# Another order of the first loads and of the first value portions in a two-layer decoder

## The chip, the core and the metric

The kernel runs on one core of a Trainium2 chip. A core has four engines that compute, each with its own list of instructions that it works off in order: TensorE (PE, matrix products), VectorE (DVE), ScalarE (ACT) and GpSimd (POOL). They wait for one another through semaphores. A fifth, SyncE (SP), does nothing here but ask for transfers between the chip's memory and the on-chip memory; ACT asks for some as well. Both share 16 DMA engines. The results of matmuls land in a small accumulation memory (PSUM) of eight banks, and have to be read out by ACT or DVE before a bank can be used again.

The metric is the time of one execution on the device, in microseconds (us); lower is better. Several executions of the kernel are timed, and one more is recorded by the profiler.

## The reference

The reference is a decoder of two layers over four batches of 256 tokens with 256 features, and a context of 1601 vectors of 256 features per batch. Cut to what matters here:

```python
x = x + L0_attn(layernorm(x))             # causal self-attention, 16 heads of 16
x = x + L0_xattn(layernorm(x), ctx, mask) # attention over the 1601 context vectors
x = x + L0_ffn(layernorm(x))              # ternary weights, 256 -> 1024 -> 256
x = x + L1_attn(layernorm(x))             # gated recurrence in chunks of 32
x = x + L1_xattn(layernorm(x), ctx)       # 16 heads of 128, 4 groups of keys and values
x = x + L1_ffn(layernorm(x))              # 8 experts, 2 per token
```

Inside `L1_xattn` the keys and values come from the context and the tokens together:

```python
kv_in = concatenate([context_hidden, draft_hidden], axis=1)   # 1601 + 256 rows
k = (kv_in @ Wk.T).reshape(b, total_len, KVH, HD)
v = (kv_in @ Wv.T).reshape(b, total_len, KVH, HD)
```

The values of the context rows depend on nothing but inputs. So they can be computed at any time before the second layer's attention over the context.

## The kernel before

**Two parts.** In the first part (to about 500 us) the four batches pass through the first layer and the recurrence. In the second part the 32 pairs of heads of the second layer's attention over the context follow one another, with the experts worked in between.

**An order written by hand, and a scheduler.** Each stage of a batch is a Python generator that emits a few instructions and yields. The loop at the end of the kernel counts ticks: in each tick every batch that has begun (`START`: batch 0 at tick 0, then at ticks 3, 8 and 13) takes one step, and then the fillers take theirs. A scheduler in the build then sets the order of each engine's instructions out of what was emitted. `behind(gen)` takes one step of a generator, and holds each compute instruction of this step behind the last one emitted before it on the same engine (`keep_behind`). This fixes an order alone and adds no wait.

**Value portions.** The filler that the change touches is `values_ahead(False)` (`ahead`, lines 323 to 349). It first asks for the value weights `wv` (two transfers of 256 KB, in runs of 512 bytes). Then for each context chunk of three batches (four chunks a batch: three of 512 rows and a last one of 65) it asks for the transposed chunk `vcT` (512 KB, into one of three buffers), and works through its portions of 128 rows. A portion is the product `vah` = chunk times `wv` on PE (L344, written as two products, which the profile shows as four matmuls of 512 columns), the copy `vst` out of PSUM by ACT (L347), and a store `v` to memory asked for by SP (L348). There are 13 portions per batch, 39 in all. `FILL` (line 42) tells how many the loop draws in a tick: two in each of the ticks 1 to 13, then one in each, up to tick 33. The first draw also issues the requests for `wv` and the first chunk.

**The start of a batch.** `self_attention(b)`: tick 0 takes the mean and variance of the tokens `x` (L244, L245), and a power on POOL (L268). Tick 1 makes the normed tokens `xh` on ACT (L296). Tick 2 transposes them on PE (`tp_sa`, L304), and DVE and ACT scale the result into `xqkv` (L431, L433). Ticks 3 and 4 make queries and keys (`pq` on PE, L441), which DVE adds to a bias (`qk`, L445). Then values (`pv`, L451; `values`, L456), and, mostly on DVE, the rotation and norm of queries and keys (L469 to L493). Then two transposes (`tp_q`, `tp_k`), a small product for the mask (`xpm`, L620, which needs `mf`, L615), and, for four quarters of the heads in turn, scores (`sc`, L525 and L531), maxima (`mx`, L535), exponentials (`sm`, L543), transposes (`tpp`, `tpq`; copied by ACT into `pT`, L552), the product with the values (`po`) and a last transpose (`tb`, L577).

**First requests.** Before the loop, SP is asked for the tokens of batch 0 (`x`, 256 KB), the weights `wqkv` (768 KB), the tokens of batches 1 to 3 (256 KB each) and `wo0` (256 KB); ACT is asked for the constants `cst` in two pieces (193 and 388 KB), `cols` (11 KB), the broadcast `rows` in two pieces (384 and 256 KB) and two rows of norm weights (`qnw` and `knw`, 64 KB each). The requests of both engines go round over eight completion semaphores, so that each waits until the request eight places before it has landed.

**PSUM.** Portions, transposes and small products draw their banks from one ring of four (`p1`); a bank comes free when the fourth one before has been read out. The scores of a quarter take two double banks (`p2`).

Of the kernel before, what the change touches and what calls it, by code (L numbers as in the profile page):

```python
# [10 lines left out]
F32 = mybir.dt.float32  # L11
# [9 lines left out]
P = 128  # L21
# [8 lines left out]
NKV, REP, HD1 = 4, 4, 128  # L30
# [8 lines left out]
LATE = tuple((3, i) for i in range(4))  # L39
LTICK = 80  # L40
WTICK = 34
FILL = {t: 2 if t < 14 else 1 for t in range(1, 34)}
SIDEN = 2
RATE = 1
START = (0, 3, 8, 13)
# [70 lines left out]
def decoder_kernel(ctx: ExitStack, tc: tile.TileContext, at, t, out):  # L116
# [3 lines left out]
    const = ctx.enter_context(tc.tile_pool(name="const", bufs=1))  # L120
# [16 lines left out]
    def p1(name):  # L137

        ring[0] += 1
        if psb and ring[0] % 3 == 0:  # L140
            return psb[0].tile([P, 512], F32, tag="one", name=name, bufs=2)
        return psa.tile([P, 512], F32, tag="one", name=name, bufs=4)
# [25 lines left out]
    def db(name):  # L168

        return wk.tile([P, 1024], F32, tag="db", name=name, bufs=NDB)  # L170
# [20 lines left out]
    def load_x(b):  # L191
        nc.sync.dma_start(out=xs[b], in_=t["x"][b].rearrange("(j p) d -> p j d", p=P))

    n_const = t["consts"].shape[1]
    cst = const.tile([P, n_const], F32, tag="cst", name="cst")
    soon = at["ones"][0]

    def load_consts(lo, hi):
        nc.scalar.dma_start(out=cst[:, lo:hi], in_=t["consts"][:, lo:hi])
# [25 lines left out]
    def row(r, name):  # L225
        o, n = _ROWS[name]
        nc.scalar.dma_start(out=r[:, 0:n], in_=t["rows"][:, o : o + n].to_broadcast([P, n]))
        return r[:, 0:n]
# [78 lines left out]
    def w512(tag, name):  # L307
        return fr.tile([P, 512], F32, tag=tag, name=name, bufs=2 if tag == "ropu" else NROPE)

    def odd(tag, name):  # L310
        return fr.tile([P, 2 * FF], F32, tag=tag, name=name)
# [7 lines left out]
    def units(i):  # L319

        return (4, 512) if i < 3 else (1, S2 - 12 * P)

    def values_ahead(late):

        if late:
            wv = [fr.tile([P, 512], F32, tag="sum", name=f"wvl{c}", bufs=2) for c in range(2)]
        else:
            w = odd("w3", "wv")
            wv = [w[:, 512 * c : 512 * (c + 1)] for c in range(2)]
        for c in range(2):  # L330
            nc.sync.dma_start(
                out=wv[c].rearrange("p (g n) -> p g n", g=NKV),
                in_=t["wkv1"][c * P : (c + 1) * P].rearrange("p (g two n) -> p g two n", g=NKV, two=2)[:, :, 1, :],
            )
        for b, i in (LATE if late else EARLY):
            n, w = units(i)
            cT = db(f"vcT{b}{i}")[:, 0 : 2 * w].rearrange("p (c n) -> p c n", c=2)
            nc.sync.dma_start(out=cT, in_=t["ctxT"][b][:, i * 512 : i * 512 + w].rearrange("(c p) n -> p c n", p=P))
            kept_values[b, i] = dram.tile([n, P, 512], F32, tag=f"v{b}{i}", name=f"v{b}{i}")
            for k in range(n):  # L340
                r = min(P, w - k * P)
                pv = p1(f"vah{b}{i}{k}")
                for c in range(2):
                    T.matmul(pv[0:r, :], lhsT=cT[:, c, k * P : k * P + r], rhs=wv[c], start=c == 0, stop=c == 1)  # L344
                nm = f"vst{b}{i}{k}"
                st = w512("rope", nm)
                A.copy(st[0:r, :], pv[0:r, :])  # L347
                nc.sync.dma_start(out=kept_values[b, i][k, 0:r, :], in_=st[0:r, :])  # L348
                yield


    def fw(name, k, n, eng, tag):
        n0 = (k // P) * n
        w = w512(tag, name) if n0 == 512 else fr.tile([P, n0], F32, tag=tag, name=name)
        return weight(w, name, 0, k, 0, n, eng)
# [3 lines left out]
    for lo, hi in ((0, 768), (768, 1280)):  # L359
        nc.scalar.dma_start(out=rows[:, lo:hi], in_=t["rows"][:, lo:hi].to_broadcast([P, hi - lo]))  # L360
    bqkv, bo, dtb = rows[:, 0:768], rows[:, 768:1024], rows[:, 1024:1280]
    for b in range(1, B):
        load_x(b)
    load_consts(soon, n_const)
    wo0 = fw("wo0", D, D, nc.sync, "rope")
    qnw, knw = (row(const.tile([P, HD1], F32, tag=n, name=n), n) for n in ("qnw", "knw"))
    identb = fr.tile([P, P], BF16, tag="identb", name="identb")
    G.tensor_copy(identb, ident)

# [7 lines left out]
    def shared_weights():  # L377

        for w in (first_weights["wfc"], first_weights["wpj"]):
            nm = f"g{len(gam)}"  # L380
            w2 = w.rearrange("p c n -> p (c n)")
            part = sm([P, 1], "gpart", f"part{nm}")
            V.tensor_reduce(part, w2, AX.X, ALU.add, apply_absolute_value=True)
            pg = p1(f"pg{nm}")
            T.matmul(pg[:, 0:1], lhsT=cc("ones"), rhs=part, start=True, stop=True)
            gw = fr.tile([P, 1], F32, tag=nm, name=nm)
            V.tensor_scalar(gw, pg[:, 0:1], 1.0 / (FF * D), None, ALU.mult)
            hi = sm([P, 1], "ghi", f"hi{nm}")
            V.tensor_scalar(hi, gw, 1e-6, 0.5, ALU.add, ALU.mult)
            lo = sm([P, 1], "glo", f"lo{nm}")  # L390
            V.tensor_scalar(lo, hi, -1.0, None, ALU.mult)
            gam.append(gw)
            yield
            for i in range(2):
                wi = w2[:, i * 1024 : (i + 1) * 1024]
                neg = db(f"neg{nm}{i}")
                V.tensor_scalar(neg, wi, lo, None, ALU.is_lt)
                V.scalar_tensor_tensor(wi, wi, hi, neg, ALU.is_gt, ALU.subtract)
                yield
        hmr = fr.tile([P, 2, 16], F32, tag="hmr", name="hmr")  # L400
        nc.scalar.dma_start(out=hmr, in_=t["hmrep"])
        for c in range(2):
            V.tensor_mul(
                kron[:, c, :].rearrange("p (m d) -> p m d", d=16), hmr[:, c, :, None].to_broadcast([P, 16, 16]),
                cc("dmask")[:, None, :].to_broadcast([P, 16, 16]),
            )
        yield
# [653 lines left out]
    def run(gen):  # L1061
        for _ in gen:
            pass
# [184 lines left out]
    def before_head(b, g):  # L1248

        if g == 0:  # L1250
            if b == 0:
                yield from angles(b)
            yield from tables(b)
        late = None
        for i in (1, 2, 3):
            gen = prep_kv(b, g, i)
            next(gen)
            yield
            if late:
                run(late)  # L1260
                yield
            late = gen
        run(late)
        yield "context"
        late = None
        if g == 0:
            normed_tokens(b)
            bt[b]["xh"] = bt[b]["centred"]()
            yield
            token_features(b)  # L1270
        for gen in (prep_q(b, g, 0), prep_q(b, g, 1), prep_kv(b, g, 0)):
            next(gen)
            yield
            if late:
                run(late)
                yield
            late = gen
        run(late)
# [215 lines left out]
    first = before_head(0, 0)  # L1494
    first_weights = {}
    tern = shared_weights()
    ahead, late = values_ahead(False), values_ahead(True)
    gens = [before(b) for b in range(B)]
    work = steps()
    through, tick, step, said = [False] * B, 0, 0, None  # L1500
    while not all(through):
        for b, gen in enumerate(gens):
            if tick >= START[b] and not through[b]:

                stage = (behind if b and tick < START[b] + 2 else next)(gen, "through")
                through[b] = stage == "through"
                if stage == "attended" and b == B - 1:

                    win = fw("win", D, 768, nc.sync, "w1")
                    wout = fw("wout", D, D, nc.sync, "rope")  # L1510
                    second_part()
        for _ in range(FILL.get(tick, 0)):
            next(ahead, None)
        if tick >= LTICK:
            next(late, None)
        if tick == WTICK:
            run(ahead)
            first_weights["wfc"] = fw("wfc", D, FF, nc.sync, "w3")
            first_weights["wpj"] = fw("wpj", FF, D, nc.sync, "w4")
        if tick >= TERN:  # L1520
            behind(tern)
        if through[0] and psb:
            if said != "first":
                said = next(first, "first")
            else:
                for _ in range(RATE):
                    if step < 8 and through[1 + step // 4]:
                        step = next(work) + 1
        elif tick >= SIDE and tick % SIDEN == 0 and said != "context":
            said = behind(first)  # L1530
        tick += 1
# [76 lines left out]
```

## Time and profile before

| what | us |
|---|---|
| median of three timed executions | 1777.13 (1775.59 to 1780.58) |
| the profiled execution's own time | 1775.81 |
| its span, first to last instruction | 1774.0 |
| busy: PE | 1708.0 (96%) |
| busy: DVE | 1300.2 (73%) |
| busy: ACT | 994.4 (56%) |
| busy: POOL | 867.2 (49%) |

The page divides the span into 40 equal slices of 44 us; each digit is the busy share of an engine in tenths. The first six slices of PE and of the DMA engines:

| slice | 1 | 2 | 3 | 4 | 5 | 6 |
|---|---|---|---|---|---|---|
| PE, tenths | 6 | 9 | 8 | 9 | 9 | 8 |
| DMA share, tenths | 6 | 3 | 2 | 1 | 2 | 3 |
| GB/s moved | 229 | 118 | 82 | 60 | 78 | 97 |

PE is the busiest engine in the sum, and almost without a gap in the second part. A share over the whole span says nothing of a single stage, though: whether a change in the first part counts is read from the waits of that part, and from what PE does at the times named. Times in the views run from the first instruction of the execution. "Idle before" is the time in which an engine had nothing to do ahead of an instruction, with what ended it; "issue" there means that the profile shows no wait that explains it. The clock column is the share of PE's full clock that was granted.

### The profile page before, as it was taken

To read this page: it belongs to the slowest core of one execution; us is meant where nothing else is said; L and a number is where in the kernel's file an instruction comes from. 1 tells how busy PE (TensorE), PEld (TensorE's weight loads), DVE (VectorE), ACT (ScalarE), POOL (GpSimd) and SP (SyncE) were. 2 spreads that over 40 slices of the span, in tenths; PEclk is the share of its full clock that TensorE was granted. 3 is DMA by queue.
4 is the path that set the end of the run, shared out by engine and by line. 5 is a ranking of instruction groups with operands and counts; after the bars stand their busy time and mean duration, and the time that the engine had idled before them with its cause. 6 is when DMAs were issued, how large, how long until landed. Compare 5 with 4: busy or idle time off the path is not lost.

```text
span 1774.0 us, 20918 instructions
## 1 busy us (share of the span) xinstructions
PE 1708.0 (96%) x6792; PEld 1014.8 (57%) x6792; DVE 1300.2 (73%) x2420; ACT 994.4 (56%) x1741; POOL 867.2 (49%) x719
## 2 busy tenths in 40 slices
PE   6989989988999999999999999999999999999998
PEld 3545668755555555555555656555555555555557
DVE  3663475789658778787787788787778778777675
ACT  2457653555556756567565556656555556655551
POOL 1210023311116677666776565676665656667460
PEclk9999999999999999999999999999999999999999
DMA  6321234201141111121211212131212213111102
GB/s 229 118 82 60 78 97 129 75 6 46 63 134 47 45 60 35 53 59 52 64 40 60 69 42 75 39 102 32 68 46 65 70 35 110 31 51 46 54 1 66
DMA packets 106565, 116.91 MB, mean 66 GB/s; under 512 B 9664, under 2 KB 80468, under 8 KB 106456
## 3 DMA queue, kind: packets, MB, share of 16 engines
q1 hardware_dynamic: 105160, 114.02, 21.0%
q10 hardware_dynamic: 1296, 1.54, 0.3%
q8 instruction: 55, 0.90, 0.2%
q14 instruction: 54, 0.44, 0.1%
HBM read 101.38 MB, written 14.16 MB: 65 GB/s over the span
## 4 chain that ended last, share of the span: by engine, by line
PE 74%; DVE 8%; ACT 7%; POOL 6%; issue 3%; DMA 1%; ACTq 0%; POOLq 0%; SPq 0%; DVEq 0%
PE bpo L1350 19%; PE bsc L1304 19%; PE pk L1233 7%; PE vah L344 4%; POOL sum L1341 3%; PE bpw L1376 3%; PE mph L1008 3%; ACT s L1329 2%; PE pq L1194 2%; ACT s L1305 2%; PE xpo L695 1%; PE mpe L1021 1%; PE xsc L650 1%; PE sc L531 1%; PE tpk L1244 1%
## 5 line engine op out<-in xcount | busy, mean ns | idle before, releaser
L1341 POOL TENSOR_TENSOR sum<-sum,s 128x512 f32<-128x512 f32 (+1 forms) x411 | 533.5, 1298 | 84.8 <-ACT s L1329 59.0
L1304 PE MATMUL bsc<-qTb,kTb 128*128 128x512 f32 (+1 forms) x960 | 457.5, 597 | 2.3 <-ACT kTb L1246 2.3
L1350 PE MATMUL bpo<-s,vb 128*128 128x512 f32 (+1 forms) x960 | 458.8, 596 | 0.0
L1305 ACT ACTIVATE s<-bsc,kn 128x512 f32<-128x512 f32 (+1 forms) x480 | 317.4, 684 | 232.3 <-PE bsc L1304 217.4
L1309 DVE SCALAR_TENSOR_TENSOR acc<-bsc,kn,acc 128x512 f32<-128x512 f32 x448 | 334.3, 746 | 103.3 <-ACT s L1305 88.5
L1326 DVE TENSOR_TENSOR s<-s,bc 128x1024 f32<-128x1024 f32 (+1 forms) x256 | 289.8, 1145 | 14.5 <-PE bc L1322 14.4
L1329 ACT ACTIVATE s<-s 128x1024 f32<-128x1024 f32 (+1 forms) x256 | 256.4, 1006 | 51.7 <-DVE s L1326 50.0
L1304 PEld LDWEIGHTS bsc<-qTb,kTb 128*128 128x128 f32 (+1 forms) x960 | 174.3, 187 | 186.1 <-issue 134.6
L1350 PEld LDWEIGHTS bpo<-s,vb 128*128 128x128 f32 (+1 forms) x960 | 169.1, 191 | 131.8 <-issue 129.5
L1151 POOL TENSOR_TENSOR ropek<-ropek,ropuk 128x512 f32<-128x512 f32 (+1 forms) x64 | 77.0, 1203 | 182.4 <-DVE ropuk L1146 181.3
L1332 POOL TENSOR_TENSOR sum<-s 128x512 f32<-128x512 f32 x32 | 40.9, 1277 | 186.4 <-ACT s L1329 186.4
L1233 PEld LDWEIGHTS pk<-wkv,cTk 128*128 128x128 f32 x832 | 101.6, 192 | 9.2 <-issue 4.5
L1158 ACT ACTIVATE ropeq<-ropeq,rnq 128x128 f32<-128x128 f32 x128 | 41.2, 390 | 113.3 <-POOL rnq L1154 109.7
L1233 PE MATMUL pk<-wkv,cTk 128*128 128x128 f32 x832 | 103.3, 275 | 0.0
L344 PE MATMUL vah<-wv,vcT 128*128 128x512 f32 (+1 forms) x156 | 79.4, 646 | 13.8 <-DMA vcT<-in_ctxT 10.1
L1307 DVE TENSOR_SCALAR acc<-bsc,kn 128x512 f32<-128x512 f32 x32 | 24.0, 750 | 64.8 <-ACT s L1305 64.8
L1376 PEld LDWEIGHTS bpw<-wo,aT 128*128 128x128 f32 x256 | 49.6, 194 | 34.5 <-issue 23.5
L1154 POOL TENSOR_TENSOR kn<-ssk,nhalf 128x4 f32<-128x4 f32 (+1 forms) x64 | 64.9, 1014 | 8.9 <-DVE ssk L1153 8.9
L347 ACT COPY vst<-vah 128x512 f32<-128x512 f32 (+1 forms) x52 | 30.3, 588 | 69.0 <-PE vah L344 50.9
L1376 PE MATMUL bpw<-wo,aT 128*128 128x256 f32 x256 | 67.3, 387 | 0.0
L1151 POOL TENSOR_TENSOR ropeq<-ropeq,ropuq 128x512 f32<-128x512 f32 x32 | 43.8, 1368 | 47.5 <-ACT s L1305 35.5
L1144 ACT ACTIVATE squares<-pk 128x256 f32<-128x256 f32 (+1 forms) x128 | 47.1, 372 | 31.8 <-PE pk L1233 28.0
(500 smaller groups left out, 2545.2 us busy)
## 6 DMA issues: line engine op xcount, KB each, us to landing
cTk<-in_ctxT SPq DMA_DIRECT2D x32, 512.0 KB
v<-vst SPq DMA_DIRECT2D x48, 256.0 KB
vb<-v SPq DMA_DIRECT2D x48, 256.0 KB
wq<-in_wq SPq DMA_DIRECT2D x16, 512.0 KB
wo<-in_wo SPq DMA_DIRECT2D x16, 512.0 KB
wi<-in_wi SPq DMA_DIRECT2D x32, 256.0 KB
vcT<-in_ctxT SPq DMA_DIRECT2D x12, 512.0 KB
xcT<-in_ctxT SPq DMA_DIRECT2D x12, 512.0 KB
```

Of the source, the lines that this page charges most:

```text
L344: T.matmul(pv[0:r, :], lhsT=cT[:, c, k * P : k * P + r], rhs=wv[c], start=c == 0, stop=c == 1)
L1151: G.tensor_tensor(r4, r4, u4[:, :, ::-1, :], ALU.add)
L1154: G.tensor_tensor(rn, ss[:, 0:n], nhalf[:, 0:n], ALU.pow)
L1233: T.matmul(pk[:, q, 0:w], lhsT=src, rhs=e["wkv"][:, c, 0:w], start=c == 0, stop=c == 1)
L1304: T.matmul(pc[0:n, :], lhsT=e["kT"][:, k * P : k * P + n], rhs=q, start=True, stop=True)
L1305: A.activation(s[0:n, i, :], pc[0:n, :], AF.Copy, scale=e["kn"][0:n, k : k + 1])
L1309: V.scalar_tensor_tensor(self.acc[0:n, :], pc[0:n, :], e["kn"][0:n, k : k + 1], self.acc[0:n, :], ALU.mult, ALU.max)
L1326: V.tensor_tensor(s[0:n, 0:w, :], s[0:n, 0:w, :], self.bc[0:n, None, :].to_broadcast([n, w, 512]), ALU.subtract)
L1329: A.activation(s[0:n, 0:w, :], s[0:n, 0:w, :], AF.Exp)
L1341: G.tensor_tensor(self.sum[0:n, :], self.sum[0:n, :], s[0:n, i, :], ALU.add)
L1350: T.matmul(self.po, lhsT=e["v"][0:n, k, :], rhs=self.s[c][0:n, i, :], start=k == 0, stop=k == NCH - 1)
L1376: T.matmul(pw[:, j * 256 : j * 256 + 256], lhsT=aT[:, o : o + P], rhs=e["wo"][:, self.h + h, :], start=True, stop=True)
```

## The change

Three edits. First, the generators `ahead` and `late` are made early, and `ahead` is started (`next(ahead)`) ahead of the loads of the other batches' tokens and of `wo0`. It gains a `yield` behind the request for the very first chunk, so that this first step issues only the requests for `wv` and chunk 0 of batch 0. ACT's second piece of constants and the two norm rows stand ahead of it in the text. Second, `FILL` begins at tick 2 instead of 1 and gives two portions up to tick 14 instead of 13. As all 39 portions are still to be drawn when the loop begins, each comes one tick later, and the last one at tick 27 instead of 26. Third, in the ticks below 6, that is for the first eight portions, the loop takes the step by `behind`.

```diff
-FILL = {t: 2 if t < 14 else 1 for t in range(1, 34)}
+FILL = {t: 2 if t < 15 else 1 for t in range(2, 34)}
...
         for b, i in (LATE if late else EARLY):
             n, w = units(i)
+            first = not (late or b or i)
             cT = db(f"vcT{b}{i}")[:, 0 : 2 * w].rearrange("p (c n) -> p c n", c=2)
             nc.sync.dma_start(out=cT, in_=t["ctxT"][b][:, i * 512 : i * 512 + w].rearrange("(c p) n -> p c n", p=P))
             kept_values[b, i] = dram.tile([n, P, 512], F32, tag=f"v{b}{i}", name=f"v{b}{i}")
+            if first:
+                yield
             for k in range(n):
...
     bqkv, bo, dtb = rows[:, 0:768], rows[:, 768:1024], rows[:, 1024:1280]
+    load_consts(soon, n_const)
+    qnw, knw = (row(const.tile([P, HD1], F32, tag=n, name=n), n) for n in ("qnw", "knw"))
+    ahead, late = values_ahead(False), values_ahead(True)
+    next(ahead)
     for b in range(1, B):
         load_x(b)
-    load_consts(soon, n_const)
     wo0 = fw("wo0", D, D, nc.sync, "rope")
-    qnw, knw = (row(const.tile([P, HD1], F32, tag=n, name=n), n) for n in ("qnw", "knw"))
...
     tern = shared_weights()
-    ahead, late = values_ahead(False), values_ahead(True)
     gens = [before(b) for b in range(B)]
...
         for _ in range(FILL.get(tick, 0)):
-            next(ahead, None)
+            (behind if tick < 6 else next)(ahead, None)
```

## The prediction

> **What bounds the kernel now.** I read the page first (PE busy 96% of the span), then the busy time by stages, then the timeline of the first 190 us. Columns of the stage rows: stretch, its length, then busy us and count of PE, PEld, DVE, ACT, POOL, granted clock, DMA share, GB/s.
>
> ```profile
> 10.00:20.00 10.00, 3.40 (x4) 1.50 (x5) 0.00 (x0) 0.00 (x0) 1.24 (x1) 1.00 1.06 348
> ...
> 160.00:200.00 40.00, 39.20 (x286) 23.61 (x285) 12.77 (x34) 28.01 (x76) 0.00 (x0) 1.00 0.16 50
> ...
> 500.00:1700.00 1200.00, 1190.08 (x4312) 673.77 (x4311) 934.13 (x1512) 713.62 (x1190) 751.47 (x610) 1.00 0.19 56
> ```
>
> From 500 us on PE idles 10 us in 1200: a gain must come from before, by PE being given the same work sooner. PE's idle time there is what can be won: about 15 us ahead of the first large matmul (16.60 less the 1.44 busy before), and some waits after it. The timeline (start, duration, then in brackets the idle time before it and who ended it), first SP's requests:
>
> ```profile
> 1.74 4.66 SPq L192 DMA_DIRECT2D x<-in_x  x3
> 8.61 0.37 SPq L235 DMA_DIRECT2D wo<-in_wo  x1
> 9.83 1.94 SPq L331 DMA_DIRECT2D wv<-in_wkv  x2
> 11.81 1.64 SPq L338 DMA_DIRECT2D vcT<-in_ctxT  x3
> ```
>
> then PE's matmuls:
>
> ```profile
> 16.60 6.29 PE L344 MATMUL vah<-wv,vcT 128*128 128x512 f32 x8 [10.08 <-DMA vcT<-in_ctxT]
> 22.72 0.60 PE L304 MATMUL tp_sa<-cst,xh 128*128 128x128 f32 x4
> 23.16 3.60 PE L344 MATMUL vah<-wv,vcT 128*128 128x512 f32 x8
> 26.59 1.89 PE L441 MATMUL pq<-wqkv,xqkv 128*128 128x256 f32 x8
> ```
>
> Two things stand here. PE waits until 16.60 for the first context chunk, which SP asks for only at 11.81, behind three token loads and wo0. And batch 0's transposes, whose operand xh was done at 9.5, stand behind the first two portions of values (8 matmuls) and start at 22.72; DVE, which can do nothing for it meanwhile, gets its first sum of q and k (qk, L445) at 28.52. The later waits of PE:
>
> ```profile
> 62.24 0.20 PE L620 MATMUL xpm<-cst,mf 13*128 13x13 f32 x1 [2.89 <-DVE mf L615]
> ...
> 95.72 1.95 PE L344 MATMUL vah<-wv,vcT 128*128 128x512 f32 x4 [1.33 <-issue]
> ...
> 103.48 3.52 PE L344 MATMUL vah<-wv,vcT 128*128 128x512 f32 x4 [2.39 <-ACT pT L552]
> ...
> 125.64 0.48 PE L525 MATMUL sc<-trib,identb 128*128 128x384 bf16 x2 [2.91 <-ACT sm L543]
> ```
>
> **Part 1, the requests.** The new order on SP is x0, wqkv, both halves of wv, chunk 0, x1, x2, x3, wo0, chunk 1. Eight completion semaphores go round over all requests, so each waits for the one eight before: the slot of x3, issued at 6.02 when cols has landed, becomes chunk 0's. So the request goes out 5.8 us earlier, but the bytes count: x1 to x3 and wo0, 1024 KB or 1.05 MB, no longer go ahead of it. From 12 to 14 us the engines moved 319 GB/s: 1.05 / 0.319 = **3.3 us**. The first portion starts at 16.60 - 3.3 = 13.3.
>
> What is pushed back is covered. x1 is asked for at 8.61 (when the first row constants have landed) instead of 1.74, and is there 0.8 us behind chunk 0, near 14; its first reader, the statistics at 29.13, moves to about 22. Without that cover the price would be what of x1 is late, one for one. x2, x3 and wo0 are read from 52 us on. Chunk 1 has the same bytes ahead as before. In the built order SP's later lines shift by a few: a mask load that waits for DVE comes ahead of batch 2's first chunk, asked for at 76.54 and used at 95.72, 19 us of cover; wherever the stores of values move, no reader waits for them before the cross-attention. On ACT the loads keep their order. DVE's and POOL's orders are unchanged, instruction for instruction.
>
> Here a rule speaks against the change. The Trainium skill ("DMA: Bandwidth & Descriptors", section Queues, rings and completion order) says that each DMA engine takes turns between the queues packet by packet. wv comes in 512-byte packets, and in its new place it meets ACT's queue, with rows and constants in packets of 2 to 3 KB: wv then gets a seventh of the bytes. The row: by the trace's landing events x1 (256 packets of 1 KB) took from 6.75 to 9.99 beside ACT's queue, while the two halves of wv (512 packets each) took 0.66 and 0.70 us with that queue nearly empty. If bytes bind, who takes turns with whom is no matter, as ACT's bytes are ahead of chunk 0 in both kernels (its last landing is 12.4): 3.3 us stay. If the packet binds, at x1's 12.7 ns each, wv takes 1024 x 12.7 = 13.0 us from 6.75, and chunk 0, 256 packets, 3.2 more: 22.9. I take 3.3, because the engines moved 340 to 400 GB/s in most of that stretch; the other end is the slow rival.
>
> **Part 2, the transposes first.** They take 0.44 us (22.72 to 23.16) and go into PE's idle time near 9.6: -0.44. PE's stream of work so moves by 3.3 + 0.44 = **3.7 us**. ACT's and DVE's xqkv are done by about 12.5, ahead of chunk 0.
>
> **Part 3, the portions later.** In PE's built order each step of the batches now stands two portions earlier: after the transposes, portions 0 and 1, then the first pq, where before four portions came first. Two portions are 8 matmuls, 3.44 us (23.16 to 26.59). So qk on DVE (28.52) moves by 3.7 + 3.44 = **7.2 us**, to 21.3, and the second one (33.68) likewise. From 33.7 to 62 DVE is busy almost without a gap, and PE's wait of 2.89 at 62.24 is for the end of just that run of work: it moves by 7.2 and keeps its length. PE's clock starts cold in both (six of the eight matmuls from 16.60 at 0.85 instead of 0.43): no difference.
>
> **The two portions are owed.** Where they are paid decides. The built order puts one of them ahead of the scores of batch 0's second quarter (97.51), the other (the last, 65 keys, 1.72 us like the rest) behind the tb transposes near 183.7; after that both orders run alike. The first: before, PE then waits 2.39 us until 103.48 for ACT's pT, which stands behind an exponential, which waits for DVE's maxima at 101.47. DVE came there 2.4 us after the scores were done (99.1), kept by batch 2's work. DVE is 7.2 earlier; the scores only 7.2 - 1.72, thus done at 93.6, still ahead of DVE's 94.3. So 1.72 of the 2.39 us of waiting are filled: no price. The wait of 1.33 at 95.72, for the bank that DVE's values addition (94.87) frees, stays and now holds a portion of batch 1. The second: PE is full from 172 to 186, so +1.72; the waits of 0.19 and 0.32 at 186.67 and 188.81, for exponentials whose scores come ahead of the late portion, take up 0.5 of it.
>
> **Sum:** -7.2 + 1.7 - 0.5 = **-6.0 us**; the same from PE's idle time: 3.7 at the start, 1.7 + 0.5 later. Bounds: nothing absorbed -3.7, all absorbed -7.2. The profiled execution took 1775.81 (span 1774.0), so 1769.8; it stands 1.3 below the median of the three runs shown, which gives 1777.13 - 6.0 = **1771.1**.
>
> A second rule weighs here. "TensorE: Matmul & The Clock Gate", section Part 1, has the array fall to half clock after an idle window of about 3.4 us. The row:
>
> ```profile
> 103.40:107.00 3.60, 3.52 (x8) 1.05 (x12) 0.93 (x3) 3.23 (x10) 0.00 (x0) 0.55 0.02 5
> ```
>
> Here a wait of 2.39 us was enough: the next 3.6 us ran at 0.55. By the rule the shorter wait saves nothing more; by the row a wait of 0.7 may spare 0.45 x 3.6 = 1.6 us: -7.6. As the wait of 1.33 just before drew no half clock, and the others of near 3 did, the threshold lies between; but a window's phase is chance, so I leave it out of the sum.
>
> **Rivals.**
> - *Paid in full*: both portions fill nothing, -3.7: 1773.4. For it: PE is full where the second is paid. Against: DVE, not PE, ended the 2.39.
> - *One half-clock stretch less*: -7.6, 1769.5. For it the row above.
> - *Hidden anyway*: a later stage waits for something that didn't move, 0: 1777. PE does wait for DVE and ACT at 245 to 262 and at 365 to 445; but these chains begin with the same PE work. That the portions are not moved as said is ruled out by the built order.
> - *Slower*: wv's small packets, chunk 0 at 22.9, that is +6.4 on the first portion; less 0.44, 1.7 and 0.5 it makes +3.8: 1781. It turns slower than before once chunk 0 lands more than 2.6 us later than now, after 19.1. For it: x1's row, and a dip to about 200 GB/s near 7 us. Against: wv's own 0.66 us.
>
> **How the numbers follow.** Chances: -6.0 half, half-clock 0.22, paid in full 0.14, hidden 0.06, slower 0.08. 0.3% (5.3 us; about what a measurement of this kernel can tell from no change) puts the border at 1771.8, close to the forecast, with about 1.5 us of scatter: faster 0.66 of the first, 0.9 of the second, a fifth of the third, 0.56 in all. Slower by over 5.3 us is the far end of the slow rival, other mishaps with it: 0.06. The rest, 0.38, is within. The range 1767 to 1776 holds the first three and the scatter.
>
> **What would show it.** Right: the first vah at 13.3, tp_sa near 9.6, qk near 21.3, the wait at 62.24 at about 55 with its length, the wait for pT cut to about 0.7, PE some 6 us earlier near 200. Wrong: chunk 0 beyond 16; DVE waiting for x1; a new wait of PE between 13 and 60; or a shift at 200 that is gone by 500.

## The result and the profile after

| | median us (lowest to highest), runs |
|---|---|
| before, on that chip | 1780.51 (1774.79 to 1781.73), 8 |
| changed | 1771.44 (1769.89 to 1773.39), 8 |
| changed against before | ratio 0.9962, 95% interval 0.995 to 0.9974: 6.8 us less (4.6 to 8.9) |
| profiled execution of the changed kernel | 1771.45, span 1769.6 (before: 1775.81 and 1774.0) |

The forecast time of 1771.1 us lies among the runs of the changed kernel, and the forecast gain of 6.0 us in the interval. The 107 timed runs of the kernel before, over all comparisons, reach from 1772.85 to 1784.82 us and crowd near 1774 and near 1780 us (granted clock 0.992 and 0.987 of full in most of them), so that its median, and every ratio here, depends on the mix: its first three runs had 1777.13. A second comparison gave the changed kernel 0.9966 (0.9953 to 0.9979), 6.0 us less. The gains here and below are worked out from the ratio and the median of the kernel before; the difference of the two medians is another number (9.1 us in the table above).

The timeline of the changed kernel, SP's first requests (start, duration, engine, line, what is asked for):

```profile
1.74 3.14 SPq L331 DMA_DIRECT2D wv<-in_wkv  x2
6.20 0.37 SPq L339 DMA_DIRECT2D vcT<-in_ctxT  x1
8.25 2.54 SPq L192 DMA_DIRECT2D x<-in_x  x3
11.11 0.37 SPq L235 DMA_DIRECT2D wo<-in_wo  x1
```

wv and the first chunk now stand where the other batches' tokens stood; the chunk is asked for at 6.20 instead of 11.81. PE's matmuls in the same timeline:

```profile
9.26 1.39 PE L304 MATMUL tp_sa<-cst,xh 128*128 128x128 f32 x4 [2.63 <-ACT xh L296]
13.51 5.49 PE L347 MATMUL vah<-wv,vcT 128*128 128x512 f32 x8 [2.86 <-DMA vcT<-in_ctxT]
18.84 1.89 PE L446 MATMUL pq<-wqkv,xqkv 128*128 128x256 f32 x8
...
54.46 0.20 PE L625 MATMUL xpm<-cst,mf 13*128 13x13 f32 x1 [2.89 <-DVE mf L620]
89.67 3.67 PE L347 MATMUL vah<-wv,vcT 128*128 128x512 f32 x8 [1.37 <-DVE values L461]
97.39 1.98 PE L347 MATMUL vah<-wv,vcT 128*128 128x512 f32 x4 [0.63 <-ACT pT L557]
117.91 0.48 PE L530 MATMUL sc<-trib,identb 128*128 128x384 bf16 x2 [2.91 <-ACT sm L548]
...
178.00 1.90 PE L347 MATMUL vah<-wv,vcT 128*65 128x512 f32 x4
...
180.62 0.50 PE L530 MATMUL sc<-trib,identb 128*128 128x384 bf16 x2
184.54 0.48 PE L530 MATMUL sc<-trib,identb 128*128 128x384 bf16 x2 [0.70 <-ACT sm L548]
```

The transposes sit in the idle time ahead of the first chunk, two portions ahead of the first pq, not four; the chunk comes 3.1 us sooner. Of the later waits, the one for the mask (2.89) kept its length, the one for pT went from 2.39 to 0.63, and a wait of 0.70 stands at 184.54. Two stages of the changed kernel (length, then busy us and count of PE, PEld, DVE, ACT, POOL, clock, DMA share, GB/s):

```profile
97.30:101.00 3.70, 3.61 (x24) 1.93 (x25) 0.93 (x3) 3.70 (x12) 0.00 (x0) 1.00 0.33 121
...
500.00:1700.00 1200.00, 1190.04 (x4306) 672.81 (x4305) 936.16 (x1514) 713.81 (x1190) 754.99 (x613) 1.00 0.19 56
```

The first runs at full clock, where before the same place had 0.55. The second is as before: the gain was made ahead of 500 us and only carried through.

DVE's order is the same in both kernels, so its instructions, taken pair by pair, say where the gain stands. In the two profiled executions the changed kernel is ahead by 7.76 us at the first qk (28.52 to 20.76), by 6.09 at 63 us, 7.73 at 102, 6.09 at 140, 4.25 at 184 to 192, and by 4.4 at the end. Which of these steps belong to the change is what the experiments had to tell, since PE's clock fell to half in different places: for 30.7 us in all before and 41.0 us after, the cold start (PE's first matmuls, before full clock is granted) and the end of the span not counted.

### The profile page after: what moved, and what is told of

Same layout as the page of the kernel before. It is cut to its first block, busy times and chain, and to the rows that moved or that the text cites. A ratio compares the mean times of both kernels' runs of the same rounds, so it can differ in the third digit from the quotient of the medians.

```text
span 1769.6 us, 20922 instructions
## 1 busy us (share of the span) xinstructions
PE 1712.0 (97%) x6792; PEld 1017.1 (57%) x6792; DVE 1299.4 (73%) x2420; ACT 994.3 (56%) x1741; POOL 866.6 (49%) x719
## 4 chain that ended last, share of the span: by engine, by line
PE 75%; DVE 8%; ACT 7%; POOL 6%; issue 2%; DMA 1%; ACTq 0%; POOLq 0%; DVEq 0%
PE bpo L1355 19%; PE bsc L1309 19%; PE pk L1238 7%; PE vah L347 4%; POOL sum L1346 3%; PE bpw L1381 3%; PE mph L1013 3%; ACT s L1334 2%; PE pq L1199 2%; PE xsc L655 2%; ACT s L1310 2%; PE xpo L700 1%; PE mpe L1026 1%; PE sc L536 1%; PE tpk L1249 1%
## 5 line engine op out<-in xcount | busy, mean ns | idle before, releaser
L1331 DVE TENSOR_TENSOR s<-s,bc 128x1024 f32<-128x1024 f32 (+1 forms) x256 | 289.5, 1143 | 15.2 <-PE bc L1327 15.1
```

Source lines behind the costliest of these rows:

```text
L1331: V.tensor_tensor(s[0:n, 0:w, :], s[0:n, 0:w, :], self.bc[0:n, None, :].to_broadcast([n, w, 512]), ALU.subtract)
```

## The experiments

All were timed beside the kernel before. Diffs are against the changed kernel.

| kernel | median us | ratio to before (95%) | us against before |
|---|---|---|---|
| requests alone | 1774.3 | 0.9985 (0.9975 to 0.9995) | -2.7 |
| portions alone | 1774.23 | 0.9982 (0.9974 to 0.9989) | -3.2 |
| one tick more | 1771.23 | 0.9961 (0.9946 to 0.9976) | -6.9 |
| all masks a step later | 1781.15 | 1.0024 (1.0013 to 1.0034) | +4.3 |
| values ahead of wqkv | 1766.98 | 0.9945 (0.993 to 0.996) | -9.8 |
| two token loads ahead again | 1772.22 | 0.9976 (0.9967 to 0.9985) | -4.3 |
| not held | 1771.98 | 0.9971 (0.9961 to 0.9981) | -5.1 |
| batch 0's mask later | 1768.37 | 0.9951 (0.9936 to 0.9965) | -8.7 |
| values ahead, batch 0's mask later | 1766.46 | 0.9942 (0.9925 to 0.9959) | -10.3 |
| changed kernel again | 1771.21 | 0.9966 (0.9953 to 0.9979) | -6.0 |

The kernel before had medians of 1777.78 (the first four rows), 1775.55 (the next four) and 1775.73 (the last two). The last column of a row is its ratio, less one, times that median.

### The two halves apart

Requests alone: the loop draws the portions as before.

```diff
-FILL = {t: 2 if t < 15 else 1 for t in range(2, 34)}
+FILL = {t: 2 if t < 14 else 1 for t in range(1, 34)}
...
-            (behind if tick < 6 else next)(ahead, None)
+            next(ahead, None)
```

> The requests of the change alone: wv and chunk 0 ahead of the other tokens, but the portions drawn from tick 1 and not held, so that PE's order is that of before. Theory (two separate shares): the first portion starts near 13.5 us instead of 16.60, everything behind it moves by the same 3.1 us and nothing is absorbed later: -3.1 us against before, ratio 0.9983, half-clock stretches apart (they come by 1.7 us each). Rival A (the request is all of it): -6.7 us, as with the whole change. Rival B (the order is all of it, the early chunk is hidden): 0.

Portions alone: the request for wv and chunk 0 goes back behind the other loads.

```diff
-    next(ahead)
     for b in range(1, B):
         load_x(b)
     wo0 = fw("wo0", D, D, nc.sync, "rope")
+    next(ahead)
```

> The later portions alone: PE's order is that of the changed kernel, but wv and chunk 0 are asked for behind wo0 as before. Theory: first portion at 16.6; the transposes near 9.3; qk on DVE 0.44 + 3.44 = 3.9 us earlier than in before (near 24.6); one of the two owed portions fills the wait that ends at 103.48 in before, the other is paid near 183: -0.44 - 1.7 = -2.2 us against before, ratio 0.9988. Rival A (the request is all): 0. Rival B (the order is all): -6.7 us.

PE in the timeline of the requests alone:

```profile
13.23 5.15 PE L347 MATMUL vah<-wv,vcT 128*128 128x512 f32 x8 [7.15 <-DMA vcT<-in_ctxT]
...
100.32 2.63 PE L347 MATMUL vah<-wv,vcT 128*128 128x512 f32 x4 [2.40 <-ACT pT L557]
```

and in that of the portions alone:

```profile
9.13 1.40 PE L304 MATMUL tp_sa<-cst,xh 128*128 128x128 f32 x4 [2.48 <-ACT xh L296]
16.93 6.13 PE L347 MATMUL vah<-wv,vcT 128*128 128x512 f32 x8 [6.40 <-DMA vcT<-in_ctxT]
...
99.77 1.98 PE L347 MATMUL vah<-wv,vcT 128*128 128x512 f32 x4 [0.63 <-ACT pT L557]
```

The start of the first portion belongs to the requests alone (13.23 against 16.93), the filled wait for pT to the portions alone (0.63 against 2.40). As far as intervals of about 2 us can tell, the shares add, 2.7 + 3.2 = 5.9 us against 6.0 and 6.8 for the whole, so neither half carries the change by itself. The 2.2 us expected of the portions alone lie inside their interval (2.0 to 4.6).

Where the 3.2 us come from, the trace and the times say differently. Pair by pair on DVE the portions alone are ahead of the kernel before by 3.69 us at the first qk, by 5.35 at 110, by 3.76 at 138 and by 1.91 at 186. The step of 1.66 up is not the filled wait, which only pays for the portion put into it: it is the half-clock stretch after the 2.39 us wait, absent here. The 1.6 us down are the next stretch, 6.83 us long at 120.87 where the kernel before had 3.41 at 127.68, and the last 1.84 the second portion. From 460 us on nothing is left: the profile stands 0.2 to 0.5 us behind.

The times gain all the same, at their upper end: on that chip the kernel before took 1772.85 to 1784.82 us (59 runs, 36 of them above 1776.2), the requests alone 1772.29 to 1780.68 (22 runs, 7 above) and the portions alone 1772.49 to 1776.11 (22 runs, none above). So the portions alone win next to nothing at the lower end; what they win is that the highest times no longer come. Whether the unfilled wait for pT made those is not shown: one profile of each kernel can't say it.

### The dose of the requests

```diff
+    ahead, late = values_ahead(False), values_ahead(True)
+    next(ahead)
     wqkv = fw("wqkv", D, 768, nc.sync, "w1")
...
-    ahead, late = values_ahead(False), values_ahead(True)
-    next(ahead)
     for b in range(1, B):
```

> The changed kernel, with wv and context chunk 0 asked for one place further ahead: in front of wqkv (768 KB), directly behind batch 0's tokens. Nothing else moves; PE, DVE, ACT and POOL keep their order. Theory A, the bytes ahead of the chunk decide when PE's first portion begins: 0.79 MB at 319 GB/s are 2.5 us, the first vah goes from 13.5 to 11.0 (no sooner than the transposes' end at 10.7), wqkv comes 3.3 us later but its first reader pq stands behind the portions, so the whole gains 2.5 more: ratio to the kernel before 0.9948. Theory B, ACT's constants and rows, asked for at the same time, decide: the first vah stays within 0.5 us of 13.5, ratio 0.996. Theory C, pushing wqkv back makes pq wait: PE idle ahead of pq, ratio 0.997 or above.

The other way, two token loads go ahead of it again:

```diff
-    next(ahead)
     for b in range(1, B):
         load_x(b)
+        if b == 2:
+            next(ahead)
```

> The changed kernel, with the tokens of batches 1 and 2 (512 KB) asked for ahead of wv and chunk 0 again, those of batch 3 and wo0 still behind. The dose is half of Part 1. Theory A, bytes: 0.52 MB at 319 GB/s put the first vah 1.6 us later, at 15.1; ratio to the kernel before 0.9971. Theory B, the moment of the request decides, and only the full move takes the chunk across to an early semaphore place: the first vah either at 13.5 as in the changed kernel or near 17 as in the kernel before, ratio 0.9962 or 0.998.

With the values ahead of wqkv, the timeline shows:

```profile
9.67 1.39 PE L304 MATMUL tp_sa<-cst,xh 128*128 128x128 f32 x4 [3.61 <-ACT xh L296]
11.36 5.74 PE L347 MATMUL vah<-wv,vcT 128*128 128x512 f32 x8 [0.30 <-DMA vcT<-in_ctxT]
16.94 1.89 PE L446 MATMUL pq<-wqkv,xqkv 128*128 128x256 f32 x8
```

With the two token loads ahead, SP's request for the chunk and PE's first portion:

```profile
9.95 0.39 SPq L339 DMA_DIRECT2D vcT<-in_ctxT  x1
...
15.46 5.82 PE L347 MATMUL vah<-wv,vcT 128*128 128x512 f32 x8 [4.92 <-DMA vcT<-in_ctxT]
```

The first portion starts at 11.36, 13.51, 15.46 and 16.60 us with none of the movable loads ahead of the chunk, with wqkv, with wqkv and two token loads, and with all of them. The bytes theory had said 11.0, 13.3 and 15.1 for the first three. From first to last the start moves 5.24 us for 1.83 MB, 350 GB/s; the single steps are uneven (366, 269 and 460 GB/s). The request of the half dose was made 3.75 us later than in the changed kernel, yet the portion started only 1.95 later; and between the two profiles of the changed kernel the request moved by 1.36 us (6.20 and 4.84, the second shown below) and the start by 0.04. So bytes, not the moment of the request, set the start. wqkv, pushed back, cost nothing: pq shows no wait.

The kernel with the values ahead of wqkv beats the changed one: 1766.98, where that has 1771.21 on the same chip. Of these 4.2 us the earlier start explains 2.15 (13.51 less 11.36). Pair by pair on DVE it is 2.7 us ahead of the changed kernel's second profile at the first qk, 3.6 from 28 to 420, 6.6 at 450, where the changed kernel has more half clock, and 4.5 at 492, behind a wait of DVE for a DMA of 2.60 us (0.46 in the changed kernel). Its profile has 23.9 us at half clock against 41.0 and 37.5 in the two of the changed kernel. Its PE waits 0.30 us for the chunk behind the transposes, so on this side little is left.

### The portions still later, and the hold

One tick more (two more portions late; pq then runs in the idle time before the chunk):

```diff
-FILL = {t: 2 if t < 15 else 1 for t in range(2, 34)}
+FILL = {t: 2 if t < 16 else 1 for t in range(3, 34)}
...
-            (behind if tick < 6 else next)(ahead, None)
+            (behind if tick < 7 else next)(ahead, None)
```

> The changed kernel with all portions one tick later still (ticks 3 to 15 draw two, held behind in the ticks below 7). The first queries and keys (pq, 1.9 us warm) then stand ahead of portion 0 on PE and need only wqkv. Theory: they run from 12.2 us in the idle time before chunk 0 (there at 13.4), so PE's work starts 1.3 us sooner than in the changed kernel, the first qk on DVE comes near 16 instead of 20.76, and four portions instead of two are owed; those that find no wait to fill are paid: between -1.3 and -4.7 us against the changed kernel, -2 taken, so -8.7 against before, ratio 0.995. Rival A (only chunk 0's arrival counts): as the changed kernel, 0.9962. Rival C (the portions owed come back as new waits): slower than the changed kernel.

```profile
11.11 3.47 PE L446 MATMUL pq<-wqkv,xqkv 128*128 128x256 f32 x8 [0.64 <-DVE xqkv L436]
14.42 3.60 PE L347 MATMUL vah<-wv,vcT 128*128 128x512 f32 x8
...
113.50 0.80 PE L530 MATMUL sc<-trib,identb 128*128 128x384 bf16 x2 [2.91 <-ACT sm L548]
```

That is its timeline. qk comes another 6.15 us earlier (14.62), but against the changed kernel's first profile DVE keeps only 4.6 of them at 100 us, 3.0 at 150, 2.5 at 300, and is 0.2 to 0.5 behind from 450 on. Against the second profile, which has the same two stretches at half clock near 424 and 438, it keeps 1.1 to 1.5 from 250 us to the end. Most of the portions owed are paid where PE is full; of the later waits named here only the one of 0.70 at 184.54 is gone. The time is that of the changed kernel. So the late draw does not pay by making qk early; it pays by what of the debt falls into a wait.

Without the hold:

```diff
-            (behind if tick < 6 else next)(ahead, None)
+            next(ahead, None)
```

> The changed kernel without the hold (plain next in the ticks below 6). PE's order differs only at the start: the first product of portion 0 stands between the first and the last of batch 0's transposes. Theory A, the hold itself is worth next to nothing because the later draw already puts the transposes ahead: the last transposes wait for chunk 0 (13.5) instead of running at 9.3, xqkv is then later by about 5 us but pq, its reader, stands behind portion 1; ratio 0.9962 to 0.9968. Theory B, the hold is what carries Part 2: pq and qk move back by 2 us or more, ratio 0.9975 or above.

```profile
9.46 0.48 PE L304 MATMUL tp_sa<-cst,xh 128*128 128x128 f32 x1 [3.29 <-ACT xh L296]
13.26 2.07 PE L347 MATMUL vah<-wv,vcT 128*128 128x512 f32 x2 [3.33 <-DMA vcT<-in_ctxT]
15.13 0.84 PE L304 MATMUL tp_sa<-cst,xh 128*128 128x128 f32 x3
```

Its timeline shows three of the four transposes behind the first product of a portion again, but the first pq (19.76) stands only 0.12 later than in the second profiled execution of the changed kernel, shown below (19.64). The time, 0.9971, cannot be told from 0.9966; the hold is worth less than these runs can show.

### The wait for the mask that stayed

PE's wait of 2.89 us at xpm moved with DVE and kept its length. Taking every batch's key mask one step later was to fill it:

```diff
-        key_mask(b)
         a = fa(b, f"a{b}").rearrange("p (j d) -> p j d", j=2)
         yield
+        key_mask(b)
```

> The changed kernel with key_mask called one step later, so that two portions stand between tp_k and xpm on PE. In before and after alike PE waits 2.89 us there for mf, and half clock follows (6.8 us of it in the profile after). Theory (a portion is worth what it fills): the wait is filled by 3.44 us of portions that are done anyway, xpm comes 0.55 later, and one or two half-clock stretches are spared (1.7 us each): -3 to -6 us against the changed kernel, ratio to before 0.994. Rival D (DVE's chain is the bound here and PE's wait is only its shadow): the same wait comes again at the scores, and the time is that of the changed kernel, 0.9962.

It did fill it, and lost, 10 us against the changed kernel. Its timeline and two of its stages (columns as above):

```profile
111.68 0.25 PE L625 MATMUL xpm<-cst,mf 13*128 13x13 f32 x1 [5.03 <-DVE mf L620]
...
145.57 0.48 PE L530 MATMUL sc<-trib,identb 128*128 128x384 bf16 x2 [2.55 <-ACT sm L548]
151.62 0.28 PE L625 MATMUL xpm<-cst,mf 13*128 13x13 f32 x1 [1.81 <-DVE mf L620]
```

```profile
111.50:130.00 18.50, 17.74 (x81) 10.32 (x81) 10.61 (x33) 7.37 (x22) 0.00 (x0) 0.71 0.22 75
145.00:165.00 20.00, 17.11 (x80) 8.02 (x80) 5.35 (x16) 8.14 (x24) 0.00 (x0) 0.66 0.07 27
```

The later batches' masks had stood well; now PE waits for two of them, 5.03 and 1.81 us, and there are three long stretches at half clock: 13.65 us that begin within the first of these waits (at 108.6), 13.65 from 146.2, behind a wait of 2.55 for sm and with the second mask's wait inside, and 10.24 from 207.6, with no long wait ahead of it. Between 100 and 220 us that is 37.5 us against 6.8 in the changed kernel's first profile; if each halved PE's work, the difference would cost 15 us. So only batch 0's mask was moved, which leaves the rest of PE's order as it is:

```diff
-        key_mask(b)
+        if b:
+            key_mask(b)
         a = fa(b, f"a{b}").rearrange("p (j d) -> p j d", j=2)
         yield
+        if not b:
+            key_mask(b)
```

> The changed kernel with the key mask of batch 0 alone taken one step later, so that on PE the two portions which stood behind the mask product xpm come ahead of it; the later batches keep their place, PE's other order is the same. It fills the wait of 2.89 us at 54.46, which kept its length under the change. Theory A, a wait of PE there is a loss like any other: PE's stream moves by 2.9 from there on and keeps at least 2 of it, ratio to the kernel before 0.995 or below. Theory B, DVE sets the pace between 30 and 120 us, so that the time comes back at the next waits for it (1.37 at 89.67, 2.91 at 117.91, each grown): ratio 0.9962, same as the changed kernel. Theory C, from the run with all batches' masks later, which lost 11 us: what cost there was batch 0's mask too, ratio above 1.0.

```profile
62.88 1.15 PE L446 MATMUL pq<-wqkv,xqkv 128*128 128x256 f32 x4 [1.27 <-DVE xqkv L436]
...
86.41 3.67 PE L347 MATMUL vah<-wv,vcT 128*128 128x512 f32 x8 [1.38 <-DVE values L461]
94.12 1.99 PE L347 MATMUL vah<-wv,vcT 128*128 128x512 f32 x4 [0.63 <-ACT pT L560]
114.65 0.80 PE L533 MATMUL sc<-trib,identb 128*128 128x384 bf16 x2 [2.91 <-ACT sm L551]
```

The wait of 2.89 and the half clock behind it are gone. In their place stands a new wait, 1.27 us at 62.88, for DVE's xqkv. The three later waits have their old lengths (1.38, 0.63, 2.91) and come 3.3 us earlier each: DVE takes no more of the time back, so theory B falls, and theory C too. Pair by pair DVE is 3.3 us ahead of the changed kernel's first profile at 69 us and 3.4 at 220. Then two half-clock stretches from 421.8 on (6.83 and 3.41, where that profile had one of 3.41) cost it 3.0, and a wait of DVE for a DMA at 492.25, 2.19 us where the changed kernel has 0.46, the rest, so that it is 0.4 behind by 492. Against the second profile it is 2.4 ahead at 69, 3.0 at 450 and 1.2 to 1.6 from 492 to 1730. In time it is 1768.37 against 1771.21. The intervals of the two ratios overlap, so the gain of nearly 3 us is shown in the traces up to 400 us, and in the time only as likely.

### Both together, and the changed kernel again

The first two edits that helped (values ahead of wqkv, batch 0's mask later) in one kernel:

> The changed kernel with both steps that helped alone: wv and chunk 0 in front of wqkv, and batch 0's key mask one step later. Theory A, one wins at the start of PE's stream (2.1 us at the first vah) and the other in a wait at 54 us, different places, so they add: ratio to the kernel before 0.9945 less about 0.0015, 0.993; the first vah at 11.4, no wait above 1.5 us before 80 us and no half-clock stretch there. Theory B, DVE sets the pace from 30 us on, and with the earlier start the mask fill has nothing left to win: 0.9945 as with the requests alone.

Its timeline: the wait for the mask is gone, and those that follow keep their lengths.

```profile
11.75 5.42 PE L347 MATMUL vah<-wv,vcT 128*128 128x512 f32 x8 [0.38 <-DMA vcT<-in_ctxT]
...
82.65 3.67 PE L347 MATMUL vah<-wv,vcT 128*128 128x512 f32 x8 [1.37 <-DVE values L461]
```

A smaller new wait for DVE's xqkv (1.10 us at 59.14) stands here too. Its trace is 2.5 us ahead of that with only the values ahead of wqkv from 63 to 100 us, but 0.1 at 445 to 470, behind a longer stretch at half clock (6.83 us at 418.05 against 3.41 at 421.71) and one more; it is 2.0 to 2.4 ahead again from 492 to 1500, as only the other then waits 2.60 us for a DMA, and 0.7 at 1729; the medians differ by 0.5, less than these runs resolve. Whether the two add is left open; that either beats the changed kernel by some 4 us on the same chip is not (1766.46 and 1766.98, the highest run 1769.17, against 1771.21, the lowest 1769.01).

The changed kernel, run again without an edit:

> The changed kernel once more, unchanged, as the measure beside it on this chip, and for the place of its half-clock stretches in a second profiled execution. Expected: ratio 0.9962 as at first. If the stretches at half clock after PE's waits fall by chance, their number and lengths differ from the first profiled execution[...] while PE's order and waits agree; if they belong to fixed places, they agree too.

Its timeline has the waits of the first profile to 0.1 us up to 220 us, but:

```profile
4.84 0.39 SPq L339 DMA_DIRECT2D vcT<-in_ctxT  x1
...
13.47 6.33 PE L347 MATMUL vah<-wv,vcT 128*128 128x512 f32 x8 [2.86 <-DMA vcT<-in_ctxT]
19.64 1.89 PE L446 MATMUL pq<-wqkv,xqkv 128*128 128x256 f32 x8
```

The same matmuls took 6.33 us instead of 5.49, as PE was at half clock until 18.8 us instead of 17.1. Of the later stretches at half clock, one of 6.83 at 249.3 is missing, the one after the mask's wait is 3.41 instead of 6.83, the one near 425 is 6.83 instead of 3.41, and one of 3.41 at 438.6 is new; with these last two DVE falls back by 3.2 us between 429 and 449, from 1.6 ahead of the first profile to 1.6 behind. So they do not belong to the kernel alone: the wait that can draw one is fixed, what is drawn is not.

## Why the prediction was right, and where it was not

**Part 1, the requests: right.** Forecast 3.3 us, first vah at 13.3; 3.1 us and 13.51 measured (13.47 in the second profile). The other end of its range, packets that take turns, is refuted, and with it the slow rival: that had put chunk 0 at 22.9. The two further doses follow the bytes as well. x1 and wqkv, pushed back, delayed nothing.

**Part 2, the transposes first: right in place (9.26), too small to be measured apart** in the time. Without the hold only the first of the four transposes stands ahead of the portions.

**Part 3, qk: right.** Forecast 7.2 us to 21.3; 20.76 and 21.57 in the two profiled executions (7.8 and 7.0 us), which lie on both sides because the cold start ended at 17.1 and 18.8. The wait for the mask moved to 54.46 and 55.27 with its 2.89 us.

**The first portion owed: right.** The 2.39 us were to fall to about 0.7; 0.63, and 2.40 where the portions stay as they were. **The second: right**, 1.8 us lost between 176 and 182.

**The credit of 0.5 behind it: wrong.** The prediction said of the waits of 0.19 and 0.32 that they were "for exponentials whose scores come ahead of the late portion". In the kernel before they stood here:

```profile
186.67 0.48 PE L525 MATMUL sc<-trib,identb 128*128 128x384 bf16 x2 [0.19 <-ACT sm L543]
...
188.81 0.48 PE L525 MATMUL sc<-trib,identb 128*128 128x384 bf16 x2 [0.32 <-ACT sm L543]
```

The scores do not come ahead of the portion. In the changed kernel the late portion runs from 178.00, the scores behind it from 180.62, and DVE, which needs them for the maxima that the exponentials wait for, stood idle until then, as its timeline shows:

```profile
182.02 0.42 DVE L540 TENSOR_REDUCE mx<-sc 128x2 f32<-128x256 f32 x1 [2.82 <-PE sc L536]
```

The chain began behind the portion and moved with it. One wait of 0.70 at 184.54 stands where two, 0.51 together, stood before: nothing is absorbed. In all eight profiles with the portions as late as here and the later batches' masks in their old place it is 0.69 or 0.70.

**The half clock, left out of the sum: where it falls was no chance, what it is worth stays open.** The prediction read 1.6 us from the row at 0.55 and left them out because "a window's phase is chance". At that place the size was right: DVE's lead over the kernel before grows by 1.64 us between 63 and 102 us in the changed kernel and by 1.66 with the portions alone. And whether a stretch follows there is not chance: in all the kernels run whose wait for pT is 0.63 or 0.64 none does, and in both with 2.39 or 2.40 one does.

Whether the 1.6 us are kept is another matter. At the next long wait, 2.91 us for sm, they are lost again in the traces: the stretch there is 6.83 or 10.24 us in all nine profiles with late portions and that wait, 3.41 in the one profile of the kernel before, and 10.24 with the requests alone. If that 3.41 was a short one by chance (63 of the 107 timed runs of the kernel before took longer than the profiled one), the saving stays in the mean; more profiles of that kernel would have to tell. A third stretch differs by chance, that after the mask's wait (6.83 and 3.41 in the two profiles of the changed kernel, 3.41 before). The ledger of the first pair of profiles is -7.76 at qk, + 1.67 by 63 us (the mask's stretch), - 1.64 by 102 (the spared one), + 1.64 by 140 (the longer one), + 1.84 by 182 (the second portion) = -4.25.

**The sum, and luck.** Without the credit the sum reads -7.2 + 1.7 = -5.5 us, and with a spared stretch that stays spared -7.1. Both lie inside the two intervals (4.6 to 8.9 and 3.7 to 8.3), as -6.0 does, so the time does not choose between them. The traces that the sum was built on give less: the two profiles of the changed kernel end 4.4 and 2.8 us ahead of the profile before. The measured 6.8 and 6.0 us hold something for which the prediction has no term, the highest times, which no longer come: the kernel before took 1772.85 to 1784.82 us, the changed one 1769.01 to 1773.39, that is 3.8 us less at the lower end and 11.4 at the upper. So the causes at the start and at the wait for pT are shown, and that their sum met the mean so closely is in part luck.

**The other rivals.** Paid in full is refuted by the filled wait, though its -3.7 lies at the very end of the second interval. One half-clock stretch less came true at its place and is open in the sum. Hidden anyway, for everything at once, is refuted by the time; for what goes beyond this change it is near the truth: one tick more made qk 6 us earlier and left the time as it was.

## What to carry to other kernels

Where the first matmul waits for a load, count the bytes asked for ahead of it, and move those that have a later reader behind it; here the start followed them over four doses, 11.36 to 16.60 us, and no reader of the loads moved back had to wait. Work drawn later is owed, not saved: follow it to where it is put in again, and count as gain only what falls into a wait whose end does not itself move with that work. Of PE's waits, first take away those long enough to draw half clock, and look at what a move does to the other batches before taking it for all of them. And look at the spread of the timed runs as well as at their middle: a change can win at the upper end alone.

## What the runs showed of the hardware

In the eleven profiled executions other than that with all masks later, each of the 44 waits of PE of 2.23 us or more between 30 and 700 us came with a stretch at half clock, which began between 1.0 us before the end of the wait and 2.3 us after it. Of the waits of 1.04 to 1.82 us that stand alone none did; one of 1.69 to 2.05 us in each execution stands right behind a wait of 3.14. The rule does not hold the other way: nine stretches there have no such wait ahead of them. One is that at 249.3, behind waits of 0.69, 0.82 and 0.16; the other eight, of 3.41 us, come 13.65 us after the start of the stretch at the wait of 2.69 near 425, in just the eight executions in which that one lasts 6.83, and not in the three in which it lasts 3.41.

The stretches are 3.41, 6.83 or 10.24 us long, and in each execution all of them begin on one grid of 3.4133 us, to 0.01 of a step. The Trainium skill ("TensorE: Matmul & The Clock Gate", Part 1) has a free-running window of that length, which the grid agrees with, and half clock after at least one idle window; here waits of two thirds of it are enough, and for a wait that stands alone the border lies between 1.8 and 2.2 us. Where a wait falls on the grid differs from one execution to the next, and two profiles of one kernel differ by up to 1.7 us at one place. That is more than many edits are worth, and a single pair of profiles (here -4.4 us, and -2.8 with the second) is no measure of a change of 6 us.
